# Moving a value projection ahead in the order of work, and turning twelve blocks' normalised rows on VectorE and through memory instead of on TensorE

## The chip, the cores and the metric

The kernel runs on one core of a Trainium2 chip. Five engines of that core work at once, each through its own queue in order: TensorE (PE: matrix products, with its weight loads shown apart as PEld), VectorE (DVE), ScalarE (ACT), GpSimd (POOL) and SyncE (SP), which here issues nearly all transfers between the core's memory (SBUF) and the chip's memory (DRAM). TensorE writes only to PSUM, a small memory of eight banks. The metric is device time in microseconds (us); lower is better.

## The reference

The program is one transformer block with conditioning (adaptive layer norm), for 8 sequences of 1024 tokens, width 512, 16 heads of 32 columns, MLP width 2048, all in float32:

```
mod = silu(condition) @ Wada + bada
sh_a, sc_a, gt_a, sh_m, sc_m, gt_m = split(mod, 6)
xm = layernorm(x, g1, be1) * (1 + sc_a) + sh_a
x  = x + gt_a * attention(xm, Wqkv, Wproj, bproj)      # causal, 16 heads
xm = layernorm(x, g2, be2) * (1 + sc_m) + sh_m
x  = x + gt_m * (gelu(xm @ W1 + b1) @ W2 + b2)
```

## The kernel before, in words

**Blocks and windows.** The 8 sequences are cut into halves of 512 tokens: 16 blocks, numbered 0 to 15, block 2b being the first half of sequence b and block 2b+1 the second. The attention of an odd block looks at the keys of both halves and is about twice as much work as that of an even block. The work is written as two interleaved streams. One is attention (`attend`): for each group of four heads, scores for the row maxima (tile `sc`), the transposed scores and their exponential (tiles `st`, `pT`), and the product with v (tile `po`). The other is linear work (`linear`), a list of steps for each window w from 1 to 15, during which block w's attention runs. The table `plan` holds the steps. For window w, with n = w - 1, these are: what is left over of block n-1's MLP (`late`), `v` of block w, the output projection of block n (`proj`), the second norm of block n (`mt`), `k` and `q` of block w+1, and then the first parts of block n's MLP: `u` 0 to 3 (up, with W1) and `d` 0 to 3 (down, with W2). The step `at` makes the normalised input of block w+2 for its later k, q and v.

**The order of instructions is decided when the program is built.** While it writes instructions out, the kernel keeps its own clock of each engine (`now`, `note`, `due`) from assumed durations, and puts next on TensorE whatever thread has the shortest wait. On the chip every engine then takes its queue strictly in that order, whatever the true times are. A transfer to DRAM or back that is part of a turn is assumed to take 8000 ns each (`HOLDING`).

**Products.** k, q, v and u are done by a Strassen-like scheme (`strassen`): seven products of half size, each of four groups of four 128x32 by 128x256 matrix instructions, with sums of quarters of the input (T1 to T4, in tile `t`) made beforehand and sums of quarters of the weights kept in DRAM. Weight pieces of 256 KB stream through a ring of eight buffers (`fetch`, tile `w`): a piece's transfer is issued when the piece eight places before it has been used for the last time. SP issues these transfers, and all others, in the written order.

**The norms.** `normalize` takes a block's rows (statistics on VectorE, the power -1/2 on GpSimd, and the scaling to `hat` on ScalarE or VectorE). `modulated` then turns the rows into columns, so that features lie along partitions, and applies gain and shift (`xm`), then makes T1 to T4. There are two ways of turning. For keys in the set `by_pe`, TensorE transposes 128x128 squares against an identity into a PSUM bank (16 transposes for a block), and gain and shift are applied on the way out of the bank. For the others, `turn` is used: four 32x32-block transposes on VectorE into `xm`, one transfer of the 1 MB tile to DRAM (`held`), four transfers of 256 KB back into the same `hat` tile, and gain and shift from there. Before the change, all sixteen blocks of the second norm (keys m0 to m15) and the first two of the first norm (a0, a1) go by TensorE; the first norm of blocks 2 to 15 goes by `turn`. There is one `hat` buffer for both norms. PSUM gives one four-bank tile to scores (`st` and `sc` share it), one bank to `po`, and three to all linear work.

```
    by_pe = {f"m{n}" for n in range(NB)} | {"a0", "a1"}
    ...
            steps = late + [("v", w)] + rows_a + [("proj", n), ("mt", n), ("k", w + 1)]
    ...
        held = kept.tile([P, NTT * D], F32, tag=f"held_{turns[0] % 2}", name=f"held_{key}")
        turns[0] += 1
        nc.sync.dma_start(held, small_blocks)
        written["held", key] = now["PE"] + HOLDING
        yield [("held", key)], []
        for m in range(NTT):
            some = held[:, ts(m, D)].rearrange("(a i) d -> i a d", i=Q)
            nc.sync.dma_start(rows[ts(m, Q), :, :], some)
```

Of the kernel before, what the change touches and what calls it, by code (L numbers as in the profile page):

```python
# [22 lines left out]
def kernel(  # L23
# [42 lines left out]
    NC = D // P  # L66
# [23 lines left out]
    blocks = [(b, h) for b in range(B) for h in range(NHALF)]  # L90
    NB = len(blocks)
# [3 lines left out]
    written, left = {}, {}  # L95
    shape = [None]
    pool_spans = []
    NEVER = float("inf")
# [129 lines left out]
    def mlp_steps(n):  # L228
        return [("u", n, i) for i in range(NQ)] + [("d", n, part) for part in range(4)]
# [8 lines left out]
    late = []  # L238
    for w in range(1, NB):
        n = w - 1  # L240
        m = mlp_steps(n)
        even = blocks[n][1] == 0
        rows_a = [("rows", blocks[n][0], "a")] if even else []
        rows_m = [("rows", blocks[n][0], "m")] if even else []
        own = m[:1] + ([("load_xa", w + 2)] if w + 2 < NB else []) + m[1:3]
        own += [("norm_a", w + 2)] if w + 2 < NB else []
        if w == NB - 1:
            steps = late[:1] + rows_a + [("proj", n), ("mt", n)] + late[1:]
            steps += [("v", w)] + rows_m + own + m[3:5] + [("load_xr", w)] + m[5:6]
            late = m[6:]  # L250
        else:

            steps = late + [("v", w)] + rows_a + [("proj", n), ("mt", n), ("k", w + 1)]
            if w == 2:
                steps = late + [("v", w), ("k", w + 1)] + rows_a + [("proj", n), ("mt", n)]
            if w == 1:
                steps = rows_a + [("k", w + 1), ("proj", n), ("mt", n)]
            steps += [("q", w + 1)] + rows_m + own
            at = [("at", w + 2)] if w + 2 < NB else []
            if blocks[w][1] == 0:  # L260

                steps += m[3:5] + [("load_xr", w)]
                late = m[5:6] + at + m[6:]
            else:
                steps += m[3:5] + [("load_xr", w)] + m[5:6] + at
                late = m[6:]
        plan[w] = steps
    n = NB - 1
# [103 lines left out]
        r0 += n  # L372
    O_G1, O_BE1, O_G2, O_BE2, O_BPROJ, O_B2, O_B1, O_BADA = at

    by_pe = {f"m{n}" for n in range(NB)} | {"a0", "a1"}
    Q = P // NTT

    def hat_tile(key):
        return tmp.tile([P, NTT, D], F32, tag="hat", name=f"hat_{key}", bufs=1)

    def load_x(n):
        b, h = blocks[n]
        rows = hat_tile(f"a{n}")
        for t in range(NTT):
            some = x[b, h * TB + t * P : h * TB + (t + 1) * P, :]
            if f"a{n}" in by_pe:
                nc.sync.dma_start(rows[:, t, :], some)
            else:
                nc.sync.dma_start(rows[ts(t, Q), :, :], some.rearrange("(t i) d -> i t d", i=Q))
        return rows  # L390
# [145 lines left out]
    act_jobs = []  # L536
# [43 lines left out]
    def normalize(tiles, key, sources):  # L580

        for t in range(NTT):
            written["hat", key, t] = NEVER
        mv = small.tile([P, NTT, 2], F32, tag="mv", name=f"mv_{key}")
        rstd = small.tile([P, NTT], F32, tag="rstd", name=f"rstd_{key}")
        offset = small.tile([P, NTT], F32, tag="offset", name=f"offset_{key}")

        def statistics(t):
            st = small.tile([P, nc.vector.BN_STATS_DIM], F32, tag="st", name=f"st_{key}_{t}")
            nc.vector.bn_stats(st, tiles[:, t, :])  # L590
            nc.vector.bn_aggr(mv[:, t, :], st)
            note("DVE", 850, [sources[t]], [("mv", key)])
            if t < NTT - 1:
                return
            if alone[0]:
                root()
                for i in range(NTT):
                    apply_tile(i)
                return
            power()  # L600
            for i in range(NTT):
                act_jobs.append((lambda i=i: apply_tile(i), [("rstd", key)]))

        def root():
            nc.scalar.activation(rstd, mv[:, :, 1], AF.Sqrt, bias=eps)
# [14 lines left out]
        def apply_tile(t):  # L620
            if t == 0:
                hats[key] = to[0] = hat_tile(key) if key[0] == "m" else tiles
            xh, xt = to[0][:, t, :], tiles[:, t, :]
            reads, writes = [("rstd", key)], [("hat", key, t)]
            if (key == "a0" and t % 2) if alone[0] else sooner(reads, writes, 700, 800) == "DVE":
                nc.vector.tensor_scalar(
                    xh, xt, rstd[:, t : t + 1], offset[:, t : t + 1], ALU.mult, ALU.add
                )
                note("DVE", 700, reads, writes, port=True)
            else:  # L630
                nc.scalar.activation(
                    xh, xt, AF.Identity, bias=offset[:, t : t + 1], scale=rstd[:, t : t + 1]
                )
                note_act(800, None, reads, writes)
# [57 lines left out]
    def modulated(key, gain, shift, b, guards):  # L692
# [25 lines left out]
        for c in range(NC):  # L718
# [30 lines left out]
                note_act(780, None, [source], writes)  # L749
            if not turned:  # L750
                live[bank] = False
            if c == 1:
                nc.vector.tensor_tensor(part["T1"], part["T1"], part["B11"], ALU.subtract)
                note("DVE", 700, [at["B11"], at["T1"]], [at["T1"]], port=True)
# [1184 lines left out]
```

## Time and profile before

| what | value |
|---|---|
| time, median of 3 runs | 3539.82 us (3537.98 to 3541.86) |
| time of the profiled execution | 3542.2 us |
| its span | 3540.5 us |
| TensorE busy | 3482.5 us, 98% of the span |
| VectorE busy | 2174.2 us, 61% |
| GpSimd busy | 2074.9 us, 59% |
| ScalarE busy | 1190.1 us, 34% |
| granted TensorE clock | 0.998 |
| bytes moved | 465.96 MB, 42.9% of the DMA engines' time on SP's queue |

How to read the rows. A row of a group is: line of the kernel, engine, operation, output tile and input tiles, shapes, count, then busy time in us and mean ns of one, then the engine's idle time just before. A row of the timeline begins with start and length in us. A row of waits gives who waited for whom, us in total, times, and longest. A matrix instruction in float32 stands twice in the trace, so the sixteen instructions of one small product are x32 there; a transpose stands once.

### The profile page before, as it was taken

The page shows a single profiled execution, that of the slowest core. Times are in us where ns is not written, and L with a number is a line of the kernel's source. Part 1 is how long each engine was busy: PE and PEld are TensorE (multiplying, and loading weights), DVE is VectorE, ACT ScalarE, POOL GpSimd, SP SyncE. Part 2 cuts the span into 40 slices and gives each one's busy share as a digit, 9 for nine tenths or more (in the row PEclk, how much of TensorE's full clock was granted, in tenths as well). Part 3 has the DMA queues.
Part 4 walks back from the last instruction along what each step waited for, and adds up shares of the span by engine and source line. Part 5 has one row for each costly group of instructions (what it writes and reads, how often), then busy time and mean ns, then how long its engine had stood idle before and what let it go on. Part 6 is the DMA issues. An engine that isn't in the chain of part 4 may idle for free.

```text
span 3540.5 us, 120499 instructions
## 1 busy us (share of the span) xinstructions
PE 3482.5 (98%) x54621; PEld 1738.0 (49%) x54621; DVE 2174.2 (61%) x2383; ACT 1190.1 (34%) x1237; POOL 2074.9 (59%) x2249
## 2 busy tenths in 40 slices
PE   8999999999999999999999999999999999999999
PEld 4444445445554555545554454544545445454445
DVE  5776675564756557565675656656566556655563
ACT  2334323352333513235232342323423234232521
POOL 2667836666376664666546675366762667526660
PEclk9999999999999999999999999999999999999999
DMA  6753434335443354524445334443344533443334
GB/s 198 245 163 103 137 117 140 111 111 156 117 148 103 110 160 117 168 85 126 142 118 159 103 115 141 124 149 107 118 132 127 156 106 119 135 126 124 100 110 140
DMA packets 319555, 465.96 MB, mean 132 GB/s; under 512 B 26300, under 2 KB 176636, under 8 KB 316996
## 3 DMA queue, kind: packets, MB, share of 16 engines
q1 hardware_dynamic: 318928, 458.22, 42.9%
q8 instruction: 430, 7.05, 0.8%
q14 instruction: 81, 0.66, 0.1%
q10 hardware_dynamic: 116, 0.03, 0.0%
HBM read 412.99 MB, written 43.06 MB: 129 GB/s over the span
## 4 chain that ended last, share of the span: by engine, by line
PE 88%; DMA 4%; DVE 3%; POOL 2%; issue 1%; ACT 1%; SPq 0%; ACTq 0%; DVEq 0%; POOLq 0%
PE bank L202 61%; PE sc L1541 8%; PE po L1672 7%; PE st L1632 7%; PE st L1620 3%; DMA w<-in_L_cond_Wproj_dram 2%; PE bank L1693 2%; PE bank L735 1%; DVE mx L1556 1%; POOL pT L1762 1%; DMA w<-in_L_cond_Wada_dram 1%; PE bank L1594 0%; POOL hT L161 0%; POOL xr L161 0%; DVE sc L1553 0%
## 5 line engine op out<-in xcount | busy, mean ns | idle before, releaser
L1762 POOL TENSOR_TENSOR pT<-pT,pT 128x256 f32<-128x256 f32 (+3 forms) x1254 | 1207.2, 998 | 347.9 <-PE po L1672 181.4
L1644 ACT ACTIVATE pT<-st 128x2048 f32<-128x2048 f32 x288 | 541.0, 1879 | 1000.5 <-PE st L1632 883.3
L202 PE MATMUL bank<-w,hT 128*32 128x256 f32 x14336 | 812.3, 380 | 1.1 <-ACT rec L1702 0.9
L1556 DVE TENSOR_REDUCE mx<-sc 128x4 f32<-128x2048 f32 (+3 forms) x384 | 666.0, 1755 | 197.7 <-PE sc L1541 191.6
L202 PEld LDWEIGHTS bank<-w,hT 128*32 128x32 f32 x14336 | 450.4, 110 | 369.2 <-issue 81.4
L202 PE MATMUL bank<-xm_m,w 128*32 128x256 f32 x8192 | 499.6, 381 | 0.0
L202 PE MATMUL bank<-t_m,w 128*32 128x256 f32 x6144 | 381.2, 380 | 0.0
L1649 POOL TENSOR_SCALAR_AFFINE_SELECT pT<-pT 128x512 f32<-128x512 f32 x256 | 168.8, 677 | 346.6 <-ACT pT L1644 344.2
L202 PEld LDWEIGHTS bank<-xm_m,w 128*32 128x32 f32 x8192 | 255.7, 110 | 224.7 <-issue 62.4
L1553 DVE TENSOR_TENSOR sc<-sc,mask 128x1024 f32<-128x1024 f32 (+1 forms) x160 | 162.9, 1018 | 319.7 <-PE sc L1541 242.5
L1541 PE MATMUL sc<-kT,qT 32*128 32x512 f32 (+3 forms) x3072 | 329.1, 520 | 1.8 <-DVE mx L1556 1.1
L1672 PE MATMUL po<-pT,v 128*32 128x512 f32 (+3 forms) x3048 | 302.9, 492 | 2.0 <-POOL pT L1649 2.0
L1632 PE MATMUL st<-qT,kT 32*128 32x512 f32 (+3 forms) x3072 | 301.0, 487 | 0.0
L202 PEld LDWEIGHTS bank<-t_m,w 128*32 128x32 f32 x6144 | 190.0, 110 | 173.3 <-issue 48.5
L202 PE MATMUL bank<-xm_a,w 128*32 128x256 f32 x3968 | 249.3, 382 | 0.0
L202 PE MATMUL bank<-w,qT 128*32 128x512 f32 x2048 | 238.2, 594 | 8.7 <-DMA w<-in_L_cond_Wproj_dram 7.2
L1711 DVE RECIPROCAL rec<-rec 128x128 f32<-128x128 f32 x256 | 225.7, 920 | 31.5 <-ACT rec L1702 31.5
L1541 PEld LDWEIGHTS sc<-kT,qT 32*128 32x128 f32 x3072 | 129.3, 183 | 179.3 <-issue 73.0
L193 DVE TENSOR_TENSOR hT<-bank,u_u 128x512 f32<-128x512 f32 x192 | 129.9, 687 | 114.1 <-PE bank L202 107.4
L202 PE MATMUL bank<-t_a,w 128*32 128x256 f32 x2944 | 188.4, 382 | 0.4 <-ACT xm_m L745 0.4
L1069 ACT ACTIVATE hT<-hT,cols 128x512 f32<-128x512 f32 x256 | 164.4, 711 | 35.5 <-DVE hT L193 35.0
L202 PEld LDWEIGHTS bank<-xm_a,w 128*32 128x32 f32 x3968 | 122.7, 110 | 105.5 <-issue 32.6
(216 smaller groups left out, 3384.6 us busy)
## 6 DMA issues: line engine op xcount, KB each, us to landing
w<-in_L_cond_W_dram SPq DMA_DIRECT2D x384, 256.0 KB
w<-kept_up_S SPq DMA_DIRECT2D x256, 256.0 KB
w<-kept_down_S SPq DMA_DIRECT2D x256, 256.0 KB
w<-kept_qkv_S SPq DMA_DIRECT2D x180, 256.0 KB
w<-in_L_cond_Wqkv_dram SPq DMA_DIRECT2D x147, 256.0 KB
hat_a<-in_x_dram SPq DMA_DIRECT2D x64, 256.0 KB
xr<-in_x_dram SPq DMA_DIRECT2D x32, 512.0 KB
w<-in_L_cond_Wproj_dram SPq DMA_DIRECT2D x64, 256.0 KB
```

Of the source, the lines that this page charges most:

```text
L193: nc.vector.tensor_tensor(out, src, other, op)
L202: nc.tensor.matmul(ps[r, :], columns, rhs, start=start, stop=stop, skip_group_check=True)
L1069: nc.scalar.activation(hT[:, i, :], hT[:, i, :], AF.Gelu, bias=cols[:, O_B1 + f : O_B1 + f + 1])
L1541: nc.tensor.matmul(sc[:, j, c0 : c0 + w], qTs[n][r, gg, ts(qt, P)], keys_of(n, kh)[r, gg, :w], start=True, stop=True, skip_group_check=True,)
L1553: nc.vector.tensor_tensor(place, place, shape_of.to_broadcast(place.shape), ALU.add)
L1556: nc.vector.tensor_reduce(maxima[n, gg][:, kh, qt, :], sc[:, :, c0 : c0 + w], axis=AX.X, op=ALU.max)
L1632: nc.tensor.matmul(st[:, j, c0 : c0 + w], kT[r, gg, ts(k % NTT, P)], qT[r, gg, TB - w :], start=False, stop=True, skip_group_check=True,)
L1644: nc.scalar.activation(pT[:, :, :used], st[:, :, :used], AF.Exp, scale=scale)
L1649: nc.gpsimd.affine_select(diagonal, diagonal, pattern=[[0, HPG], [1, P]], compare_op=ALU.is_ge, fill=0.0, base=0, channel_multiplier=-1,)
L1672: nc.tensor.matmul(po[r, TB - w :], v[:, k % NTT, g * P + j * hd : g * P + (j + 1) * hd], pT[:, j, c0 : c0 + w], start=(k == 0), stop=last ...
L1711: nc.vector.reciprocal(some, some)
L1762: nc.gpsimd.tensor_tensor(into, into, pT[:, j, c0 : c0 + w], ALU.add)
```

## The change

Three things are edited. First, the value projection of odd blocks 5, 7, ..., 15 is taken out of its own window and put right behind k and q of the same block, in the even window before it (`early_v`). Second, in odd windows from 5 to 13, where no v is left at the head of the window, the output projection and the second norm of block n are put ahead of the old MLP's last part, `late[-1:]` (the step d 3 of block n-1), and k of the next block follows it; window 15 loses its v too. Third, the second norm of blocks 2 to 13 is turned by `turn` rather than by TensorE. So that it doesn't take the one `hat` buffer while a first-norm block is in it, its scaling waits in the builder's clock for a mark, `"hat free"`, set when a first-norm block's last chunk has been used. Nothing else is changed; what is computed is the same.

```diff
@@ plan, window NB - 1
-            steps += [("v", w)] + rows_m + own + m[3:5] + [("load_xr", w)] + m[5:6]
+            steps += rows_m + own + m[3:5] + [("load_xr", w)] + m[5:6]
@@ plan, other windows
             steps = late + [("v", w)] + rows_a + [("proj", n), ("mt", n), ("k", w + 1)]
+            if w > 3 and blocks[w][1]:
+                steps = late[:-1] + rows_a + [("proj", n), ("mt", n)] + late[-1:] + [("k", w + 1)]
...
-            steps += [("q", w + 1)] + rows_m + own
+            early_v = [("v", w + 1)] if w > 2 and not blocks[w][1] else []
+            steps += [("q", w + 1)] + early_v + rows_m + own
@@ which keys TensorE turns
-    by_pe = {f"m{n}" for n in range(NB)} | {"a0", "a1"}
+    by_pe = {"a0", "a1", "m0", "m1", f"m{NB - 2}", f"m{NB - 1}"}
@@ load_x
         rows = hat_tile(f"a{n}")
+        written["hat free"] = NEVER
@@ normalize
+        free = ["hat free"] if key[0] == "m" else []
...
-                act_jobs.append((lambda i=i: apply_tile(i), [("rstd", key)]))
+                act_jobs.append((lambda i=i: apply_tile(i), [("rstd", key), *free]))
@@ modulated
+            if c == NC - 1 and key[0] == "a":
+                written["hat free"] = 0.0
```

## The prediction

> **What bounds the kernel now.** I read the page's busy times first, then the busy time of the middle of the span, then what TensorE waited for, then the groups of instructions that the change touches.
>
> ```profile
> span 3540.5 us, 120499 instructions
> PE 3482.5 (98%) x54621; PEld 1738.0 (49%) x54621; DVE 2174.2 (61%) x2383; ACT 1190.1 (34%) x1237; POOL 2074.9 (59%) x2249
> ...
> 654.00:3400.00 2746.00, 2729.99 (x42664) 1362.62 (x42664) 1679.82 (x1809) 947.09 (x972) 1656.38 (x1784) 1.00 0.42 126
> ...
> PE st L1620 <- DVE mx L1556: 7.4, 6, 2.4
> PE bank L202 <- DMA w<-in_L_cond_Wproj_dram: 7.2, 9, 1.5
> ```
>
> The reader is to see that TensorE is the bound: from 654 to 3400 us (columns: the stretch, its length, then busy PE, PEld, DVE, ACT, POOL, clock, DMA share, GB/s) it is busy 2729.99 of 2746.00 us, so it stands still for 16 us. The order that the builder writes fits the chip well, and the largest waits over the whole run are 7 us. VectorE, ScalarE and GpSimd have room. So the time is TensorE's work plus its stalls: whatever leaves TensorE is gained, and every wait that is new at its head is lost.
>
> **What leaves TensorE.** Both programs' orders of instructions are equal on TensorE up to the first transpose of block 2's second norm (about 650 us in the trace); from there they differ. After the change 192 of 256 second-norm transposes are gone (12 blocks of 16), and nothing is added to it: v, projection and MLP keep their counts.
>
> ```profile
> L735 PE MATMUL bank<-ident,hat_m 128*128 128x128 f32 x256 | 46.0, 297 | 3.6 <-ACT hat_m L658 3.6
> ...
> 916.17 0.33 PE L735 MATMUL bank<-ident,hat_m 128*128 128x128 f32 x1
> 916.43 1.07 PE L202 MATMUL bank<-t_a,w 128*32 128x256 f32 x16
> 917.32 0.61 PE L202 MATMUL bank<-xm_a,w 128*32 128x256 f32 x8
> 917.87 0.66 PE L735 MATMUL bank<-ident,hat_m 128*128 128x128 f32 x4
> 918.45 1.50 PE L202 MATMUL bank<-xm_a,w 128*32 128x256 f32 x24
> ```
>
> The 256 transposes hold TensorE 46.0 us, so 12 of 16 blocks hold it 46.0 x 12/16 = 34.5 us. Starts of neighbours say the same: one transpose alone takes 916.43 - 916.17 = 0.26 us and four take 918.45 - 917.87 = 0.58 us, so 0.11 us for each and 0.15 us for the change of form; in the written order such changes fall from 1283 to 1162. That gives 192 x 0.11 + 121 x 0.12 to 0.15 = 36 to 39 us. I take 34.5. The bounds of the gain are 30 (block 3's transposes by neighbouring starts, 2.5 us, x 12) and 39.
>
> **What comes instead.** For each of the 12 blocks: four 32x32 transposes on VectorE, one 1 MB transfer out, four of 256 KB back, gain and shift from SBUF instead of PSUM.
>
> ```profile
> L671 DVE STREAM_TRANSPOSE xm_a<-hat_a 128x512 f32<-128x512 f32 x56 | 34.6, 672 | 0.0
> L745 ACT ACTIVATE xm_a<-hat_a,shifta,gaina 128x512 f32<-128x512 f32 x41 | 30.3, 804 | 47.7 <-DMA hat_a<-held_a 45.5 <-DMA out_dram<-xr 2.2
> L745 ACT ACTIVATE xm_m<-bank,shiftm,gainm 128x512 f32<-128x512 f32 x37 | 27.7, 775 | 47.6 <-PE bank L735 47.4
> ...
> 130.53 0.96 SPq L680 DMA_DIRECT2D held_a<-xm_a  x1
> 138.60 2.90 SPq L685 DMA_DIRECT2D hat_a<-held_a  x4
> 150.79 2.93 ACT L745 ACTIVATE xm_a<-hat_a,shifta,gaina 128x512 f32<-128x512 f32 x4 [5.94 <-DMA hat_a<-held_a]
> ...
> 3010.22 0.38 SPq L680 DMA_DIRECT2D held_a<-xm_a  x1
> 3017.59 3.74 SPq L685 DMA_DIRECT2D hat_a<-held_a  x4
> 3026.72 2.23 ACT L745 ACTIVATE xm_a<-hat_a,shifta,gaina 128x512 f32<-128x512 f32 x3 [5.96 <-DMA hat_a<-held_a]
> ```
>
> VectorE gets 48 x 0.67 = 32 us, 1% of its queue, beside matrix work. Gain and shift cost 0.80 instead of 0.78 us. The transfers add 12 x 2 MB = 25 MB to 466. None of this lies on the path by its amount; the delay does. From the issue of `held` to the first use of the rows that came back, the first of the trace's 14 turns takes 150.79 - 130.53 = 20.3 us and the last, which is also the shortest, 16.5; the 14 have a mean of 18.2, 8.6 to the issue of the way back and 9.6 from there. The builder assumes 8 + 8. So the new order may ask for these columns about 2 us too early.
>
> **Is the delay covered?** The moved steps are there to answer this, so I add up TensorE's written order between the last matrix instruction of a block's projection and the first of its up product u0, at the rates of the rows below (32 records in 1.72 us, a score unit of eight in 1.07 us).
>
> ```profile
> 881.25 1.91 PE L202 MATMUL bank<-xm_a,w 128*32 128x256 f32 x32
> 882.97 0.61 PE L202 MATMUL bank<-t_a,w 128*32 128x256 f32 x8
> ...
> 892.36 1.14 PE L1541 MATMUL sc<-kT,qT 32*128 32x512 f32 x8
> 893.43 1.93 PE L202 MATMUL bank<-t_a,w 128*32 128x256 f32 x32
> ...
> 922.95 1.91 PE L202 MATMUL bank<-xm_m,w 128*32 128x256 f32 x32
> ```
>
> For block 3 of the kernel before this sum is 42.7 us, and the trace has 922.95 - 881.25 = 41.7, so it can be trusted to some 2 us. It holds 24.1 us of linear work, k and q (7 products of 1.72 us each). After the change it is 36.1 us for most blocks: k, q and v for odd n, the MLP's last part (13.8 us), k and q for even n. Only block 2 keeps k and q alone. With the attention between, u0 begins 48.6, 60.5, 58.2, 54.3, 52.9, 52.7, 53.6, 47.8, 55.8, 47.8, 57.1 and 44.4 us after the projection for blocks 2 to 13.
>
> Against that stands the time at which the columns are there. In block 3 of the trace:
>
> ```profile
> 901.93 1.05 POOL L613 TENSOR_TENSOR rstd_m<-rstd_m,minus_half 128x4 f32<-128x4 f32 x1
> 908.95 0.82 ACT L631 ACTIVATE hat_m<-xr,offset_m,rstd_m 128x512 f32<-128x512 f32 x1
> 914.72 0.45 DVE L626 TENSOR_SCALAR hat_m<-xr,rstd_m,offset_m 128x512 f32<-128x512 f32 x1
> 924.84 0.68 DVE L193 TENSOR_TENSOR qT<-bank,u_q 128x512 f32<-128x512 f32 x1
> ...
> L1556 DVE TENSOR_REDUCE mx<-sc 128x4 f32<-128x2048 f32 x192 | 439.8, 2291 | 194.4 <-PE sc L1541 191.6
> ...
> SPq L340 <- PE bank L202: 1594.6, 658, 19.3
> ```
>
> The last scaled tile is ready 914.72 + 0.45 - 881.25, about 34 us after the projection, because GpSimd's power waits behind attention's sums until 901.93. In the new order VectorE's third and fourth transposes of block 3 stand behind q's last eviction (924.84, 44 us after, in the trace; its product ends at 39.5 in the new order) and behind the maxima of two score units whose products end at 42.0 and 45.7 us; the second maximum takes 2.29 us, to 48.0, and the transposes with an eviction of v between end near 50. SP issues `held` at 50.5, the turn takes 18.2 and two gain-and-shift operations 2 x 0.80: 70.3 us, against 60.5 of work. **Block 3 stalls 9.8 us.** Nothing else can fill it: the stretch from 55.5 to 60.5 is attention alone, with one buffer for scores.
>
> For the others I do the same, with one more bound. SP's queue is in order and mostly waits for TensorE to free a weight buffer (the row with 1594.6 us), so `held` and the way back cannot go out before the weight piece written ahead of them has its buffer. Block 2: `held` 30.5, ready 50.3, stall 1.7. Block 7: `held` behind a piece freed at 33.0, ready 53.0, stall 0.3. Block 11: the gain and shift stand behind an exponential that ends at 46.6, ready 48.2, stall 0.4. The rest have slack: block 5 1.4, 12 2.5, 9 2.8, 4 3.0, 6 4.3, and 10, 8 and 13 from 6.9 to 8.9. Behind the way back, the next weight piece is needed 10 us or more later, so SP's wait for `held` starves no product.
>
> A long stall has a second price. In the trace one of 2.87 us is followed by slow products:
>
> ```profile
> 3434.82 0.48 PE L735 MATMUL bank<-ident,hat_m 128*128 128x128 f32 x1 [2.87 <-ACT hat_m L658]
> 3438.49 2.96 PE L202 MATMUL bank<-xm_m,w 128*32 128x256 f32 x32
> 3441.27 1.90 PE L202 MATMUL bank<-t_m,w 128*32 128x256 f32 x32
> ```
>
> The 32 records at 3438.49 take 2.78 us to the next start instead of 1.72, and transposes before them were slow too. I price a restart at 1.5 us, once, in block 3.
>
> **The moves.** v and the projection cost nothing by themselves: same products, same pieces of weights, and the even windows that get the v have lighter attention. Their price is in what they leave bare. In window 15 no v is left, so ahead of block 14's projection 14.7 us of attention stand alone. Each of its five units needs the one score buffer until its exponential is through (1.88 us, next fence), so TensorE idles for perhaps 2 us there. Odd windows have denser attention, but in the written order the distance between users of the score buffer falls short of the exponential or the maximum only at these places (blocks 2, 3, 14).
>
> ```profile
> L1644 ACT ACTIVATE pT<-st 128x2048 f32<-128x2048 f32 x288 | 541.0, 1879 | 1000.5 <-PE st L1632 883.3 <-POOL pT L1762 62.4 <-POOL mcols L1578 24.2
> ...
>   ACT xm_a L745: 45.5, 11
>   DVE xm_a L739: 22.0, 12
> ```
>
> The turns also make ScalarE and VectorE stand in their queues until the rows are back: 45.5 us in 11 and 22.0 us in 12 waits in the kernel before, with evictions and exponentials queued behind them. With 14 such turns TensorE's stalls from 654 us on are 16 us for all reasons, 7 of them the projection's weights. For 12 more turns I take 3 us; bounds 0 and 9.
>
> **The sum.** -34.5 (transposes) + 9.8 + 1.7 + 0.3 + 0.4 (stalls at u0) + 1.5 (restart) + 2 (block 14) + 3 (queues) = -15.8 us. The profiled execution took 3542.2 us, which gives 3526.4; it lies 2.4 us above the median of 3539.82, so against the runs I say 3524 us.
>
> A page would have the turn shorter. The Trainium skill, "DMA: Bandwidth & Descriptors", section "Anatomy of one DMA — SWDGE (gpsimd) path", fits a transfer as 2.0 us plus its bytes at 436 GB/s, which for 1 MB is an estimate of 4.4 us each way, 8.8 for the turn, and would leave block 3 a stall of 0.4 us and the whole at about 3511 us. The trace does not agree: its shortest turn is 16.5 us. (The fit is for another issuing engine.)
>
> **Rivals.** (1) *The turn is longer for these blocks* than for the first norm's, whose use lies far off and whose rows are not waited for by TensorE. At +2.5 us the stalls are 4.2 + 12.3 + 2.8 + 2.9 + 1.1 for blocks 2, 3, 7, 11 and 5, 23.3 us, with four restarts 29, with the other 5 us 34: no gain. From there on the kernel is slower; at +5 us nine blocks stall, 43 us, and with six restarts and the other 5 us the time is 3562 us. For it: the second norm's turn falls where weights stream hardest, and the first turn of the trace took 20.3 us. Against: 13 of the 14 took 16.5 to 19.1 us, at a DMA share of 0.42. The skill's "VectorE: DVE Perf Modes", section "Rules for kernel authors", speaks on this side: for 128x128 transposes it says to use TensorE where a PSUM result will do. Chance 0.15. (2) *The delay is hidden everywhere*, block 3 too, because VectorE reaches the transposes earlier than the written order suggests: -34.5 + 3, 3508 us. Against it stand the two maxima queued ahead. Chance 0.10. (3) *Denser odd windows and blocked queues* cost about 1 us more per block, 12 us, in evictions that free a bank late: 3536 us. For it: the 67 us that ScalarE and VectorE wait for turned rows would nearly double. Against: they cost TensorE little so far. Chance 0.15. The forecast has 0.60.
>
> **How the numbers follow.** A measurement of this kernel tells 0.2%, 7 us, from no change. Forecast and rival 2 are faster (0.70), rival 3 splits into 0.04 faster, 0.07 same and 0.04 slower, rival 1 into 0.03 same and 0.12 slower: 0.74, 0.10, 0.16. The forecast's own range is 3515 to 3533 (stalls at u0 for turns 2 us shorter or longer on the mean). The range for 8 in 10 begins at rival 2, 3508, and reaches to 3542, just past rival 1's point of no gain; it leaves out 0.05 below and 0.14 above.
>
> **What would show it.** Right: 64 instead of 256 transposes, about 11.5 us; TensorE's longest wait ahead of block 3's first up product, near 10 us, ended by ScalarE's gain and shift, with slower products behind it; small waits at blocks 2, 7, 11; a bare stretch with gaps before block 14's projection; turns of 17 to 20 us. Wrong: waits at u0 in most blocks, or turns over 21 us (rival 1); no wait at block 3 (rival 2); many waits for banks or maxima in odd windows (rival 3).

## The result and the profile after

The changed kernel takes 3536.86 us (median of 20 runs, 3530.67 to 3543.64) against 3542.24 us for the kernel before (20 runs, 3537.98 to 3549.08). The ratio is 0.9979, 95% interval 0.9973 to 0.9986: faster by 0.21%, some 7 us. The forecast was 3524 us, a gain of 16 to 18. The profiled execution took 3537.37 us, its span is 3534.7, 5.8 less than before.

The page of the changed kernel:

```profile
span 3534.7 us, 120362 instructions
PE 3461.9 (98%) x54429; PEld 1732.1 (49%) x54429; DVE 2201.4 (62%) x2438; ACT 1208.4 (34%) x1264; POOL 2054.0 (58%) x2228
```

Its busy times in the middle (columns as in the prediction):

```profile
654.00:3400.00 2746.00, 2718.49 (x42692) 1359.38 (x42692) 1713.56 (x1869) 963.59 (x998) 1639.26 (x1764) 1.00 0.46 135
```

Span and granted clock after (0.998 before):

```profile
core 0: 3534.7 us, clock 0.995
```

Three groups of instructions, after (line numbers are 4 to 7 higher than before):

```profile
L740 PE MATMUL bank<-ident,hat_m 128*128 128x128 f32 x64 | 10.8, 301 | 3.3 <-ACT hat_m L663 3.3
L1700 PE MATMUL bank<-pT,ones 128*32 128x512 f32 (+3 forms) x536 | 76.4, 591 | 2.5 <-POOL pT L1769 2.5
L1700 PEld LDWEIGHTS bank<-pT,ones 128*32 128x32 f32 x536 | 19.6, 110 | 17.7 <-POOL pT L1769 8.2 <-issue 2.7
```

The last two groups in the kernel before:

```profile
L1693 PE MATMUL bank<-pT,ones 128*32 128x512 f32 (+3 forms) x536 | 69.4, 583 | 0.0
L1693 PEld LDWEIGHTS bank<-pT,ones 128*32 128x32 f32 x536 | 17.5, 110 | 11.7 <-issue 2.2 <-POOL pT L1762 1.1
```

The transposes went as forecast: 64 are left, 10.8 us instead of 46.0, so 35.2 us less. But TensorE stands still more (2718 busy of 2746 us in the middle, 2730 before), its clock is lower (0.995, not 0.998), and a group that the change doesn't touch, attention's row sums (`pT` times ones), holds it 76.4 us instead of 69.4.

What TensorE waited for from 654 to 3560 us, after (us in total, times, longest):

```profile
PE st L1627 <- DVE mx L1563: 4.4, 7, 1.1
PE sc L1548 <- ACT pT L1651: 3.8, 1, 3.8
PE po L1679 <- POOL pT L1656: 3.6, 3, 1.8
PE bank L1518 <- DVE mx L1535: 3.5, 3, 1.6
...
PE sc L1548 <- DVE mx L1563: 2.7, 2, 2.4
PE bank L1700 <- POOL pT L1769: 2.5, 1, 2.5
...
PE bank L202 <- DMA w<-in_L_cond_Wproj_dram: 0.9, 2, 0.6
PE bank L202 <- ACT xm_m L750: 0.8, 1, 0.8
```

and before:

```profile
PE bank L202 <- DMA w<-in_L_cond_Wproj_dram: 7.1, 8, 1.5
PE st L1620 <- DVE mx L1556: 4.6, 4, 1.6
...
PE po L1672 <- POOL pT L1649: 2.0, 1, 2.0
```

Hardly any of the new waits is at a product that needs the turned rows (`xm_m`, 0.8 us). They are in attention: for maxima (`mx`), exponentials and sums (`pT`). The waits for the projection's weights went, 7.1 to 0.9 us, which the prediction did not foresee.

The books close to under 1 us. Idle times of TensorE over 0.2 us add up to 67.7 us over the whole span against 52.9: +14.8. There are also stretches in which the granted clock is 0.50, and a product takes twice as long. These are six after (6.8, 3.4, 10.2, 3.4, 6.8 and 3.4 us) and three before (3.4, 3.4 and 6.8 us). Their sums, after and then before, start with the length and TensorE's busy time in them:

```profile
sum 34.00, PE 31.02 PEld 13.90 DVE 23.75 ACT 14.21 POOL 10.81; mean PE 5.17 PEld 2.32 DVE 3.96 ACT 2.37 POOL 1.80
```

```profile
sum 13.60, PE 12.35 PEld 5.80 DVE 7.12 ACT 7.79 POOL 4.36; mean PE 4.12 PEld 1.93 DVE 2.37 ACT 2.60 POOL 1.45
```

Half of the busy time is lost at half speed: +9.3. Row sums: +7.0, of which 1.2 are half speed already counted, so +5.8. With -35.2 that is -5.3; the spans differ by -5.8.

### The profile page after: what moved, and what is told of

It reads as the page before. It is cut to its first block, busy times and chain, and to the rows that moved or that the text cites. A ratio compares the mean times of both kernels' runs of the same rounds, so it can differ in the third digit from the quotient of the medians.

```text
span 3534.7 us, 120362 instructions
## 1 busy us (share of the span) xinstructions
PE 3461.9 (98%) x54429; PEld 1732.1 (49%) x54429; DVE 2201.4 (62%) x2438; ACT 1208.4 (34%) x1264; POOL 2054.0 (58%) x2228
## 5 line engine op out<-in xcount | busy, mean ns | idle before, releaser
L202 PE MATMUL bank<-w,hT 128*32 128x256 f32 x14336 | 822.7, 380 | 0.5 <-issue 0.5
L1563 DVE TENSOR_REDUCE mx<-sc 128x4 f32<-128x2048 f32 (+3 forms) x381 | 658.9, 1750 | 228.1 <-PE sc L1548 222.3
L202 PE MATMUL bank<-xm_a,w 128*32 128x256 f32 x3968 | 241.7, 380 | 0.0
```

Source lines behind the costliest of these rows:

```text
L202: nc.tensor.matmul(ps[r, :], columns, rhs, start=start, stop=stop, skip_group_check=True)
L1563: nc.vector.tensor_reduce(maxima[n, gg][:, kh, qt, :], sc[:, :, c0 : c0 + w], axis=AX.X, op=ALU.max)
```

## The places

**Block 3.** TensorE's instructions ahead of block 3's first up product:

```profile
935.19 1.14 PE L1548 MATMUL sc<-kT,qT 32*128 32x512 f32 x8
938.75 1.22 PE L1548 MATMUL sc<-kT,qT 32*128 32x512 f32 x8 [2.42 <-DVE mx L1563]
939.72 1.94 PE L1518 MATMUL bank<-kT,qT 32*128 32x512 f32 x6
943.29 1.22 PE L1518 MATMUL bank<-kT,qT 32*128 32x512 f32 x1 [1.63 <-DVE mx L1535]
...
947.00 3.35 PE L202 MATMUL bank<-xm_m,w 128*32 128x256 f32 x32
```

The clock there (columns as before: the stretch, its length, the five engines' busy times, then the granted clock):

```profile
939.70:949.90 10.20, 8.57 (x56) 4.14 (x53) 9.28 (x14) 2.93 (x4) 1.77 (x1) 0.50 0.18 38
```

The linear work had run out, so the builder wrote a second score unit right behind the first. It needs the one score buffer, and the maximum of the first takes 2.3 us: 2.42 us of idle time, 1.63 more, and a granted clock of 0.50 from 939.7 to 949.9 us (32 records in 3.35 us instead of 1.91). The clock falls behind the first of the two waits, before the second. The first up product itself waits for nothing. Such a unit without linear work beside it I call bare.

**Block 8.** The first norm's turn of block 8 on VectorE, SP and ScalarE, and TensorE behind it:

```profile
1476.49 1.88 DVE L676 STREAM_TRANSPOSE xm_a<-hat_a 128x512 f32<-128x512 f32 x3
...
1491.91 0.69 DVE L193 TENSOR_TENSOR y<-bank,row_ga 128x512 f32<-128x512 f32 x1 [4.29 <-PE bank L202]
...
1493.66 0.70 DVE L676 STREAM_TRANSPOSE xm_a<-hat_a 128x512 f32<-128x512 f32 x1
...
1494.39 0.32 SPq L685 DMA_DIRECT2D held_a<-xm_a  x1
...
1509.33 1.80 SPq L690 DMA_DIRECT2D hat_a<-held_a  x4
...
1518.78 2.93 ACT L750 ACTIVATE xm_a<-hat_a,shifta,gaina 128x512 f32<-128x512 f32 x4 [12.43 <-DMA hat_a<-held_a]
1521.61 1.85 ACT L1651 ACTIVATE pT<-st 128x2048 f32<-128x2048 f32 x1
...
1523.52 2.09 PE L1548 MATMUL sc<-kT,qT 32*128 32x512 f32 x8 [3.75 <-ACT pT L1651]
```

In the kernel before, this block's four transposes run in a row (1475.42 to 1477.90). Here three run, and the fourth stands 15 us behind the projection's evictions (`y`), because the moved projection now begins at once behind the old MLP's part next to which this turn was written. `held` goes out at 1494.39 instead of 1479.65, the way back is issued 14.9 us later (7.5 in the kernel before), ScalarE stands 12.43 us for the rows with an exponential queued behind it, and TensorE waits for that one.

**The end of block 15's attention.**

```profile
3404.83 1.07 PE L1679 MATMUL po<-pT,v 128*32 128x384 f32 x16 [1.77 <-POOL pT L1656]
3408.41 2.39 PE L1700 MATMUL bank<-pT,ones 128*32 128x512 f32 x8 [2.50 <-POOL pT L1769]
3410.11 16.24 PE L202 MATMUL bank<-w,qT 128*32 128x512 f32 x128
```

Window 15 has lost 12 us of linear work with its v; when the last units wait for GpSimd nothing is left to put beside them, and the clock falls (128 records of the projection in 16.24 us; 13.92 before).

## The experiments

Times are given as ratio to the kernel before in the same hour, with its 95% interval; microseconds are that ratio times 3543.

**1. The two halves of the change.** e_moves keeps the moved order and leaves all second norms on TensorE:

```diff
-    by_pe = {"a0", "a1", "m0", "m1", f"m{NB - 2}", f"m{NB - 1}"}
+    by_pe = {f"m{n}" for n in range(NB)} | {"a0", "a1"}
```

> The moved order alone: v and the projection where the changed kernel has them, all sixteen second norms still transposed on TensorE. Local theory (the full 35 us of transposes is gained, and what is lost lies at a few places): nothing is gained here, the written work is within 2 us of before, and only the bare stretch ahead of block 14's projection costs some 3 us: 3540 to 3546 us beside a before of 3542. Diffuse theory (the moves make odd windows denser and cost 0.5 to 1 us per block whatever is turned): 3548 to 3554 us.

e_turns has the changed `by_pe` and the plan of before:

```diff
-            if w > 3 and blocks[w][1]:
-                steps = late[:-1] + rows_a + [("proj", n), ("mt", n)] + late[-1:] + [("k", w + 1)]
...
-            steps += [("q", w + 1)] + early_v + rows_m + own
+            steps += [("q", w + 1)] + rows_m + own
...
-            steps += rows_m + own + m[3:5] + [("load_xr", w)] + m[5:6]
+            steps += [("v", w)] + rows_m + own + m[3:5] + [("load_xr", w)] + m[5:6]
```

> The turning alone: blocks 2 to 13 turned on VectorE, v and projection left in their old places, so that odd blocks have 24 us of linear work as cover instead of 36. Local theory: waits ahead of u0 in blocks 3, 5, 7, 11 and 12 and a little in 4 and 10, 40 us together, with about six restarts of 3 us: 44 us of written work saved less 58 lost, 3556 us, bounds 3540 and 3590, slower than the changed kernel by over 10 us and with slow products behind each wait. Rival (the cover is not needed, because VectorE takes other work in between and the rows come sooner): 3505 to 3520 us.

e_moves: 1.0015 (1.0006 to 1.0024), 5 us slower (2 to 9 by the interval), between the two expectations and close to the second: the moves are not free. The profiled executions differ by 7.5 us, and only 2.8 of that lies behind the start of block 0's first up product; the rest lies ahead of it, where both kernels have the same order and e_moves has four stretches at half speed instead of two. e_turns: 1.0126 (1.0112 to 1.0140), 45 us slower, at the far end of the bounds. Its two largest waits of TensorE from 654 us on:

```profile
PE st L1624 <- DVE mx L1560: 18.0, 13, 3.8
PE bank L1515 <- DVE mx L1532: 16.4, 10, 2.2
```

Its granted clock is 0.988. So without the 12 us of v, or of the old MLP's last part, as cover the delay is ruinous, and it shows as maxima of bare units and a lower clock, hardly as waits ahead of u0. The moves are what makes the turning possible at all. Changed kernel less moved order is 0.9979 - 1.0015, 13 us for turning; forecast were 18.

**2. Block 3, and the assumed delay.** e_m3 puts block 3's second norm back; e_hold and e_hold6500 change what the builder assumes of a transfer:

```diff
-    by_pe = {"a0", "a1", "m0", "m1", f"m{NB - 2}", f"m{NB - 1}"}
+    by_pe = {"a0", "a1", "m0", "m1", "m3", f"m{NB - 2}", f"m{NB - 1}"}   # e_m3
...
-    HOLDING = 8000
+    HOLDING = 10000   # e_hold; 6500 in e_hold6500
```

> Only block 3's second norm goes back to TensorE. Local theory: the two gaps at its first products (2.42 and 1.63 us) and the 10 us at half speed behind them go, 9.3 us; the 16 transposes and their changes of form bring 4.1 us of written work back: 5 us less than the changed kernel, 3531 to 3533 us beside its 3537, granted clock 0.997. Diffuse theory: the delay turns up at the next late block, or the slow stretch had another cause: 3537 to 3541 us.

> The builder takes 10 + 10 us for a turn's two transfers instead of 8 + 8 (measured here: 13.5 to 24.4 us for both), so it writes gain and shift further back in ScalarE's and VectorE's queues. If the other lost microseconds come from queues that stand behind rows not yet back (3.75 us at block 8 with the 3.5 us at half speed behind it, small ones at blocks 4 and 2): 5 to 8 us less than the changed kernel, 3529 to 3532 us, and fewer waits of ScalarE for returned rows. If the lost time has another cause, or if the later gain and shift now delay u0 instead: 3536 to 3542 us, with more waits ahead of u0.

> The builder takes 6.5 + 6.5 us for a turn's transfers. With 8 + 8 it leaves two score units of attention without linear work beside them at blocks 2 and 3 (3.4 us too little between users of the score buffer in the written order), with 10 + 10 six such (11.4 us), here only the one ahead of block 14's projection (0.8 us). If those bare units with the slow products behind them are what the delay costs: 4 to 8 us less than the changed kernel, 3529 to 3533 us. If the wait only moves to the first up product of block 3 (written 57.9 us after the projection, rows there at 64 to 67) and to ScalarE's queue: 3537 to 3543 us with a gap of 6 to 9 us there.

e_m3: 1.0004 (0.9995 to 1.0012), 9 us slower than the changed kernel. Block 3's waits and its slow products are gone, as expected; but behind it the builder writes another order, and there it is block 14's first-norm rows that come late:

```profile
2799.93 1.67 DVE L744 TENSOR_SCALAR xm_a<-hat_a,gaina,shifta 128x512 f32<-128x512 f32 x2 [8.02 <-DMA hat_a<-held_a]
...
2805.11 2.28 DVE L1563 TENSOR_REDUCE mx<-sc 128x4 f32<-128x2048 f32 x1
...
2807.44 0.61 PE L1627 MATMUL st<-mrow,minus_ones 32*128 32x512 bf16 x4 [5.88 <-DVE mx L1563]
```

VectorE stands 8.02 us, a maximum is queued behind, TensorE waits 5.88 us. e_hold: 1.0005 (0.9996 to 1.0014), also 9 us slower than the changed kernel: ScalarE's waits for returned first-norm rows fall from 38.5 to 14.8 us, but by the builder's assumed durations the written order falls short by 11.4 us in all between users of the score buffer (4.2 us in the changed kernel). e_hold6500: 1.0033 (1.0021 to 1.0046): no bare units but one, and the rows come late for ScalarE (12.55 us in one wait) and for VectorE, whose maximum then holds TensorE:

```profile
1535.52 0.62 PE L1627 MATMUL st<-mrow,minus_ones 32*128 32x512 bf16 x4 [6.22 <-DVE mx L1563]
```

About 11 us of it lie in the first 230 us, where the same number governs a first-norm turn. My theory that the loss sits in a few places which can be mended one by one fell here: the delay is paid in bare units if it is assumed, and in blocked queues if it is not, and every edit draws a new order.

**3. What the trips cost.** The trip through memory is left out:

```diff
         yield [("blocks", key)], []
+        if key[0] == "m":   # "a" in the other two
+            written["turned", key] = now["PE"]
+            return
```

> The changed kernel without the trip of the second norm's rows through memory: VectorE's transposes, gain and shift stay, the 1 MB out and the four pieces back are left out for blocks 2 to 13, so the columns hold wrong values. If the lost 21 us (from the moved order's 3548.5, less 34 us, to the changed kernel's 3536) are the price of the second norm's delay, nearly all of it comes back: 3515 to 3520 us, no score unit that waits bare at block 3, clock 0.997. If the first norm's turns and the moves are the larger part, only block 3's 9 us and block 4's 2.4 us come back: 3524 to 3528 us.

> The changed kernel without the trip of the first norm's rows (columns of blocks 2 to 15 wrong), the second norm's trips kept. If queues that stand behind first-norm rows cost the time (12.4 us of ScalarE's waiting and 5.5 us of TensorE's at block 8, the hat buffer freed late): 3526 to 3531 us, and no wait of ScalarE or VectorE for first-norm rows. If the second norm's delay is the cost: 3534 to 3537 us, with block 3's gaps as they were.

> The same omission in the kernel before (first norm's rows not sent out and back, columns of blocks 2 to 15 wrong): what these 14 trips cost where the second norm is on TensorE. 45 us of ScalarE's waits go, but TensorE waited for none of them: 3541 to 3544 us. If their traffic or their place in SP's queue holds up weights (7 us of waits for the projection's weights): 3534 to 3538 us.

The builder's assumed delay goes with the trip, so each of these kernels has a new written order too.

e_trip_m: 0.9963 (0.9949 to 0.9976). All twelve trips of the second norm cost 6 us with their delay (0.9979 - 0.9963, with intervals of 0.0007 and 0.0014 to each side), less than either expectation had; block 8's wait stays (3.54 us there). e_trip_a: 0.9957 (0.9944 to 0.9969), and e_trip_a_before: 0.9977 (0.9969 to 0.9986): the first norm's trips cost 8 us in both kernels, and all of it lies ahead of block 0's first up product (it begins 221.2 and 221.4 us after the start instead of 229.9 and 228.8; in the profiles of kernels with the same order up to there it begins between 227.2 and 233.5). So e_trip_a comes out at the time of its first expectation, but not for the reason given there. Those trips as such are no price of this change. Turning loses some 21 us (13 gained of 34), and by these medians 15 of them are not the second norm's trips.

**4. Where the first norm is begun, and block 15's v.** e_v15 leaves block 15's v in window 15:

```diff
-            early_v = [("v", w + 1)] if w > 2 and not blocks[w][1] else []
+            early_v = [("v", w + 1)] if 2 < w < NB - 2 and not blocks[w][1] else []
...
-            steps += rows_m + own + m[3:5] + [("load_xr", w)] + m[5:6]
+            steps += [("v", w)] + rows_m + own + m[3:5] + [("load_xr", w)] + m[5:6]
```

e_at begins the first norm's columns in windows of even blocks one part of the old MLP earlier:

```diff
-                steps += m[3:5] + [("load_xr", w)]
-                late = m[5:6] + at + m[6:]
+                steps += m[3:5] + [("load_xr", w)] + at
+                late = m[5:]
```

e_a2_at has this edit and also `"a2"` in `by_pe`; e_a2_v15_at has all three edits.

> Only block 15's v goes back behind block 14's projection; all else as in the changed kernel. If the ends of block 15's window cost what its trace shows there (four waits of 3.2 us ahead of block 14's projection, 4.3 us of waits at the end of the attention with 6.1 us at half speed behind, against 2.9 us of waits in the kernel before): 4 to 6 us less than the changed kernel, 3530 to 3533 us, no slow products near 3405. Against it: block 13's cover falls from 44.4 to 38.4 us, its rows were there after 36.2, and the written order has a bare score unit at block 13 (2.5 us short). Rival (the gain is lost again there): 3535 to 3539 us.

> In windows of even blocks the first norm's columns of the block after next are begun one part of the old MLP earlier (ahead of d1 and not behind it), so that this turn is further from the next projection. If block 8's 3.75 us of waiting behind ScalarE and its 3.5 us at half speed come from that turn (24.4 us long, spread over the projection): 4 to 7 us less than the changed kernel, 3529 to 3533 us, first-norm turns of even blocks under 20 us. If such waits only come up at other blocks: 3535 to 3539 us.

> As the run before, and block 2's first norm transposed on TensorE: without first-norm trips the time up to u0 of block 0 was 7 to 9 us shorter in both kernels, and block 2's is the only one of these trips that lies there. 16 transposes with their changes of form cost 3 us. If its trip is the cause: first 230 us shorter by 5 to 7 us after the transposes, 3525 to 3529 us. If traffic in general was the cause there: 3532 to 3538 us.

> All three edits together. If their gains are separate places: 3520 to 3526 us, below both kernels by 10 us or more. If a new written order brings new bare units elsewhere (4.7 us short in 7 places by the written order, 4.2 in 3 for the changed kernel): 3530 to 3538 us.

e_at: 0.9948 (0.9935 to 0.9960), 3524.49 us, better than expected and 11 us under the changed kernel. Block 8's turn in it:

```profile
1431.76 2.48 DVE L676 STREAM_TRANSPOSE xm_a<-hat_a 128x512 f32<-128x512 f32 x4
...
1436.43 0.38 SPq L685 DMA_DIRECT2D held_a<-xm_a  x1
...
1456.46 2.21 ACT L750 ACTIVATE xm_a<-hat_a,shifta,gaina 128x512 f32<-128x512 f32 x3
```

The transposes run in a row again and ScalarE doesn't stand. Block 3 is mended too, by the new order: its transposes end some 38 us after the projection instead of 50, and the first up product follows the score unit at once:

```profile
932.20 1.14 PE L1548 MATMUL sc<-kT,qT 32*128 32x512 f32 x8
933.27 1.93 PE L202 MATMUL bank<-xm_m,w 128*32 128x256 f32 x32
```

The other three miss. e_v15: 0.9997 (0.9988 to 1.0006); block 15's end loses its 1.77 us wait, but block 13, with less cover, gets one of 3.81 us for a maximum. e_a2_at: 0.9986 (0.9977 to 0.9994) and e_a2_v15_at: 0.9987 (0.9978 to 0.9996): the time to block 0's first up product falls by only 3 to 5 us, hardly outside the spread just given, so block 2's trip alone is not shown to be what the first 230 us pay for, and the new order behind it loses 13 us to e_at (a wait of 4.16 us behind ScalarE, which stood 11.3 us for block 6's first-norm rows, and one of 3.55 us for a maximum, behind which the granted clock is 0.50 for 20.5 us in e_a2_at).

**5. Mechanism or luck?** Small edits moved the time by up to 13 us, so e_at could be a lucky draw. The same edit was made on the moved order alone (e_moves_at) and on the kernel before (e_at_before); e_at_early starts the columns one part earlier still; e_at_trip_m leaves out the second norm's trips as in 3; e_at_v15_m13 joins the edits of e_at and e_v15 and puts block 13's second norm back; e_at_again is e_at once more.

```diff
-                steps += m[3:5] + [("load_xr", w)] + at
+                steps += m[3:4] + at + m[4:5] + [("load_xr", w)]   # e_at_early, against e_at
...
-    by_pe = {"a0", "a1", "m0", "m1", f"m{NB - 2}", f"m{NB - 1}"}
+    by_pe = {"a0", "a1", "m0", "m1", f"m{NB - 3}", f"m{NB - 2}", f"m{NB - 1}"}   # e_at_v15_m13
```

> The first norm's columns of even windows begun one more part earlier, ahead of d0. If what was lost comes from this turn being pushed against the projection, the second step earlier keeps the gain of the first: 3520 to 3529 us, no first-norm wait of ScalarE over 7 us. If the gain of the run with one step was a lucky written order (other small edits moved the time by up to 13 us): anywhere from 3530 to 3545 us.

> The moved order without turning second norms, and the first norm's columns begun one part earlier. The moved order alone cost 5 us over the kernel before; if the first norm's turn in the projection's way is its cause: 3539 to 3544 us. If the moves cost by their density: 3547 to 3551 us.

> Control: the kernel before with only this edit. There the old MLP's last part and v lie between the turn and the projection, its transposes take 2.4 us in a row, so nothing is in the way: 3540 to 3546 us. If beginning these columns earlier is worth something by itself: 3530 to 3536 us.

> The run with the columns one part earlier (3524.5 us), without the trip of the second norm's rows (columns of blocks 2 to 13 wrong): what is left of the second norm's delay. There block 3's columns are ready 57.8 us after the projection and u0 is at 56.9, and TensorE has only a 1.42 us wait for gain and shift (block 11) and 1.84 us with 3.4 us at half speed at block 12: 2 to 5 us less, 3519 to 3523 us. If hidden costs (traffic, SP's queue) remain: 3510 to 3516 us.

> Columns one part earlier, block 15's v behind block 14's projection, and block 13's second norm on TensorE, since its cover shrinks to 38 us there (3.81 us of waiting and 1.9 us at half speed in the run that moved this v alone). If the end of block 15's attention lacks cover because its v was moved: the wait of 1.77 us and the slow products there go, 5 us, for 2.5 us more written work: 3520 to 3524 us. If they stay (attention simply comes later in any kernel with less work on TensorE): 3526 to 3530 us.

> The run with the columns one part earlier, a second time, beside the one above: 3522 to 3527 us if its 18 us under the kernel before belong to the kernel; above 3530 if they belonged to that hour.

e_moves_at: 0.9977 (0.9967 to 0.9987), 13 us under e_moves and better than either expectation: with the turn out of the projection's way the moved order costs nothing. (The two profiled executions are 17.8 us apart: TensorE's waits are 10.5 us less and half speed costs 6.7 less.) In e_moves the four transposes of blocks 6 and 12 were spread over 13.2 and 15.7 us; here they take 2.5 and 6.0. Block 10's turn fell into the projection too, and its way back was issued 12.1 us after `held` (9.3 in the kernel before). TensorE waited behind it in e_moves, with 3.4 us at half speed after that:

```profile
1964.04 2.93 ACT L750 ACTIVATE xm_a<-hat_a,shifta,gaina 128x512 f32<-128x512 f32 x4 [9.54 <-DMA hat_a<-held_a]
...
1968.79 1.14 PE L1548 MATMUL sc<-kT,qT 32*128 32x512 f32 x8 [2.84 <-ACT pT L1651]
```

e_at_before: 0.9981 (0.9972 to 0.9990), 7 us under the kernel before, where I expected nothing. Its trace shows most of that: from block 0's first up product on, TensorE's waits for the projection's weights fall from 7.2 to 2.4 us. This gain can't be added to the others. In e_moves these waits are 2.4 us and in the changed kernel 1.1, so most of what the edit brings there must lie elsewhere.

e_at_early: 0.9969 (0.9958 to 0.9980) keeps 4 us of the gain, and ScalarE again stands long for first-norm rows (15.3 us at block 14). That is in the range expected for a lucky written order, so beginning this turn earlier doesn't give e_at's time by itself. e_at_again: 0.9942 (0.9929 to 0.9954): the time belongs to the kernel.

The traces of the changed kernel and of e_at say where the 12.0 us between their spans lie: TensorE's waits are 11.6 us less, half speed costs 4.4 less, the row sums 2.3 more and the transposes 0.7 more, which closes to 1 us. Block 8's wait with its half speed (3.75 + 1.6) and block 3's two waits with theirs (4.1 + 4.3) are gone, 13.7 us in all; small losses elsewhere take some back. Block 8's part is the collision. Block 3's part came with the new written order, and how much of that was luck I can't separate.

e_at_trip_m: 0.9939 (0.9926 to 0.9952), 1 to 3 us under e_at. There the second norm's delay is hidden almost entirely, and still turning brings only 0.9977 - 0.9945, some 11 us, on the better order. What it loses then is not delay. The row sums show one part of it. TensorE, its weight loads and GpSimd at 2115 us in e_at:

```profile
2114.87 2.25 PE L1700 MATMUL bank<-pT,ones 128*32 128x512 f32 x8
...
2115.24 0.14 PEld L1700 LDWEIGHTS bank<-pT,ones 128*32 128x32 f32 x2 [0.26 <-POOL pT L1769]
2115.66 0.14 PEld L1700 LDWEIGHTS bank<-pT,ones 128*32 128x32 f32 x2 [0.28 <-POOL pT L1769]
...
2109.12 6.90 POOL L1769 TENSOR_TENSOR pT<-pT,pT 128x384 f32<-128x384 f32 x8
```

Eight records that take 1.04 us when their sums are ready take 2.25 us, because GpSimd finishes the sums pair by pair while TensorE loads them. The page counts this as busy. The group holds TensorE 69.4 to 70.5 us in every kernel that keeps the second norm on TensorE (before, e_moves, e_moves_at, e_at_before) and 73.2 to 81.9 in every kernel that turns it, 78.6 with the trips left out. With less work on TensorE between them the attention units come sooner, and GpSimd, whose sums take 1214 us in all, doesn't keep up at places. That it is the shorter distance and not something else about the turning is argued from this pattern, not isolated.

e_at_v15_m13 (block 15's v back in its window, block 13's second norm on TensorE): 0.9939 (0.9926 to 0.9953), level with e_at. The end of block 15's attention in it:

```profile
3388.24 1.07 PE L1679 MATMUL po<-pT,v 128*32 128x384 f32 x16 [0.34 <-POOL pT L1656]
3389.12 3.21 PE L202 MATMUL bank<-w,hT 128*32 128x256 f32 x56
3392.14 1.22 PE L1700 MATMUL bank<-pT,ones 128*32 128x512 f32 x8
```

The old MLP's products stand between the last units and the waits of 1.77 and 2.50 us are gone with the slow stretch: that loss was the price of moving block 15's v. The time is no better since block 13's transposes, a wait of 1.77 us later in the projection and 6.8 us at half speed at block 15's own transposes (3.4 there in e_at) take it back.

Both e_at (3524.49 and 3522.33 us) and e_at_v15_m13 (3522.71 us) beat the kernel before by 18 to 22 us and the changed kernel by 11 to 14.

## Why the prediction was right or wrong

Right was the direction, the range (the time lies 13 us above the forecast in it), and what leaves TensorE: -34.5 forecast, -35.2 by the group. Right was the turn: twelve turns of the second norm took 13.5 to 20.1 us, mean 16.9, so rival 1 (a longer turn) fell. Right was the working for block 3 up to its last step: the transposes were to end near 50 us and `held` to go at 50.5, and they did at 49.7 and 50.5; idle time and slow products came to 4.1 + 4.3 = 8.4 us against 9.8 + 1.5. Only the place was wrong: not ahead of the first up product but in attention units which the builder writes bare while it waits. Blocks 7 and 11 had no wait at u0, block 2 one of 0.80 us, block 14's stretch 3.2 us of waits for 2 forecast. Counted together, the idle terms of the sum (9.8 + 1.7 + 0.3 + 0.4 + 2 + 3 = 17.2) are near the 14.8 measured, though 6 us of that is a gain at the projection's weights that was not in it.

Wrong were three steps. The first and the last of the following are terms that were too small or missing, by 7.8 and 5.8 us; the second says where part of the idle time came from. The sum of -15.8 us, with transposes 0.7 us better and waits 2.4 us smaller than summed, and with these two terms, becomes -5.3, against -5.8 measured between the spans.

- *"A long stall has a second price ... I price a restart at 1.5 us, once, in block 3."* Measured: 9.3 us more lost at half speed, in stretches of 10.2 us at block 3, 3.4 at block 8 and 6.8 at the end of block 15, and one of 6.8 us instead of 3.4 in the first 230 us. The row I took the price from was read too low: the granted clock is 0.50 there from 3433.8 to 3440.6 us, with TensorE busy for 5.55 us, so up to 2.8 us were lost. The Trainium skill, "TensorE: Matmul & The Clock Gate", section "HAM oscillation — how this bites in real kernels", puts the bound at idle gaps over about 3.4 us. The traces disagree on the bound. Behind their first 240 us every wait over 3 us was followed by a stretch at half speed, but some of 1.8 to 2.9 us were too: one of 2.42 us at block 3 and one of 2.01 us in e_moves were, one of 2.50 us in e_v15 and one of 2.93 us in e_hold were not. The same wait near the end of block 15 (2.04 us before, 2.05 in e_at_before) was followed by one only in e_at_before. The traces agree with Part 1 of that page of the Trainium skill, by which some 3.4 us of busy time bring the clock back: the stretch behind block 8's single wait is 3.4 us.
- *"The moves. v and the projection cost nothing by themselves."* They cost 5 us by the ratio of e_moves, 2.8 in its trace behind the start of block 0's first up product. Counting what was moved, I looked at products, weights and the score buffer, but not at what had stood between: the old MLP's last part and v had kept the projection's VectorE work off the first norm's transposes. Collisions of this kind are the 3.75 us at block 8 and the 2.84 us at block 10 in e_moves.
- *The row sums are in no term*, +7.0 us, 5.8 without what half speed explains. GpSimd was late for them, as the waits of the weight loads show; that the shorter distance between units made it late is argued, not isolated. I had looked for places where scores come too close; I did not ask whether GpSimd, last in attention's chain, keeps up when TensorE has 35 us less to do between units.

Rival 3 (denser odd windows and blocked queues, 3536 us) gave the time that was measured, and its mechanism is the nearest: ScalarE blocked by returned rows, GpSimd behind. But it put the cost into evictions that free a bank late, and the traces have it in exponentials, maxima and sums. Rival 2 had block 3 hidden; e_at shows an order in which it is.

Open stays how much of any kernel's difference to its neighbour is the draw of the written order. What turning loses on the better order is accounted for to some 3 us: in e_at TensorE's waits from block 0's first up product on are 9 us more than in e_moves_at, the row sums 8, the slow stretches some 4, which with -35 leaves -14; the ratios say -11.

## What to carry to other kernels

When work leaves the bounding engine, ask what it had been covering: here 35 us of transposes had also, as I read it, spaced out the attention units, and the engines at the end of that chain (GpSimd's sums, ScalarE's exponentials) became late in small steps that a profile counts as busy. When a step is moved, list what then stands next to each other on every other engine, not only on the one it leaves; and where a builder writes the order, an assumed delay costs either way, so begin the delayed step earlier (11 us here with one step, 4 with two) rather than tune the assumption (9 and 19 us lost).

## What the runs showed that I had not expected

A TensorE record group can hide waits: eight row-sum records at 2.25 us instead of 1.04, with no idle time shown on PE; the weight loads' own waits (17.7 against 11.7 us in the group, 8.2 against 1.1 of them ended by GpSimd) are the place to look. Waits of 1.8 to 2.9 us were followed by half speed in some places and not in others, and two executions of one kernel (e_at and e_at_again) had 6.8 and 3.4 us of it at the same place. In all traces a stretch lasts 3.41 us or a whole multiple of it: 6.83, 10.24 or 20.48. A gain measured in one kernel was not there to be had in its neighbour: e_at_before gained 7 us, mostly in waits that the moves had already removed. And putting one block's sixteen transposes of the first norm back on TensorE (e_a2_at), 4 us of work by the written order, moved the time by 13 us.
